# Mixing stage of a spectral layer: the filters of ScalarE and GpSimd are worked on one row ahead

## The chip, the cores and the metric

The kernel runs on one core of a Trainium2 chip. The metric is the device time of one execution in microseconds; the time of a kernel is the median over its runs. Engines are called TensorE (PE in the profile; PEld is its weight load), VectorE (DVE), ScalarE (ACT), GpSimd (POOL) and SyncE (SP), which here issues all DMAs.

## The reference

Two layers on x of shape (4, 128, 128, 128), float32: a state-space layer on windows of 8 x 8, and a spectral layer. The change touches a part of the second only. Cut to it:

```python
z = (x - mu) / sqrt(var + 1e-5) * ln_gamma + ln_beta
Xf = rfft2(z)                                  # b, d, 128, 65
Uf = Xf[:, :, None] * conj(Phi)                # 16 filters l, complex
U = irfft2(Uf)
S = einsum('bdlxy,lhd->bhxy', U, Theta)        # Theta: 16 matrices 128 x 128
H = gelu(einsum('bdxy,hd->bhxy', S, W1) + b1)
return x + einsum('bhxy,dh->bdxy', H, W2) + b2
```

The inverse transform is linear, so the kernel multiplies by Theta and sums over the 16 filters while the data are still spectra, and transforms back only the sum: for each frequency, S = sum over l of conj(Phi_l) * (Theta_l X), a complex product of a real matrix's result with a complex factor.

## The kernel before

The kernel has four stages, one after the other: `mamba_layer` (to about 7016 us of the span), `spectra` (forward transforms, to 7624), `mix` (to 9638) and `images_and_mlp` (inverse transforms and the two small matrices, to the end). Only `mix` changes.

`mix` goes over the 65 frequencies y of the halved axis, called rows here (KY is 65). A row's spectra, `xk`, are one tile of 128 channels by 4 images, 2 parts (real, imaginary) and 128 frequencies of the other axis. `load(y)` fetches it with two DMAs of 256 KB; the pool holds three such tiles, and the load of row y + 2 stands at the head of row y.

Within a row the loop runs over the 16 filters k (NL is 16). For each, TensorE makes two PSUM tiles v0 and v1 (line 578): Theta_k times the real and the imaginary part, each four matmuls of 128 x 128 x 128 in float32, one for each image. A tile fills one PSUM bank, and each of the two kinds has four buffers, so all eight banks are used. Then come four products with the factors Phi (`phi`, a column of 128 factors for every filter and row), each on 128 x 512 elements: real part from v0 and v1, imaginary part from v1 and v0.

Who works on the products depends on k:

- Ten filters are VectorE's. Line 593 makes the first two products of a row without an addition, line 595 multiplies a PSUM tile by its factor and adds the accumulator `acc`, all in one instruction.
- Six filters, APART = (1, 4, 6, 9, 12, 14), are ScalarE's and GpSimd's. ScalarE multiplies (line 589) from PSUM into a tile `part` in SBUF (eight buffers), and GpSimd adds it onto a second accumulator, `apart` in the code (line 591; the profile calls both accumulators acc). The first two products of a row are written straight into it, so a row has 24 products of ScalarE and 22 additions of GpSimd.

`finish(y)` (lines 557 to 564) adds the two accumulators of a row on VectorE (line 560, 128 x 1024) and stores the sum with eight DMAs of 64 KB. It stands behind filter 5 of the next row.

The stage has a manual schedule: every engine works through its instructions in the order in which the code writes them, and the semaphore waits between engines follow from the tiles. Which buffer of a tag a new tile gets is settled when the program is built; the pool does not simply take them in turn. A TensorE instruction that is to overwrite a bank waits for the engine that read the bank last.

Of the kernel before, what the change touches and what calls it, by code (L numbers as in the profile page):

```python
# [13 lines left out]
F32 = mybir.dt.float32  # L14
BF16 = mybir.dt.bfloat16
AF = mybir.ActivationFunctionType
ALU = mybir.AluOpType
PSUM = bass.MemoryType.PSUM

P = 128  # L20
# [6 lines left out]
W = 128  # L27
HB = 512
NL = 16
KY = W // 2 + 1  # L30
# [3 lines left out]
def mamba_layer(tc, d, x, x1, zb, deltas, dus):  # L34
# [14 lines left out]

    APART = {4: 0, 6: 2, 8: 5, 20: 12, 24: 15, 28: 18, 30: 26}  # L50
    rows_all = [(b, slice(i * WS, (i + 1) * WS)) for b in range(B) for i in range(NH)]
    R = len(rows_all)
    with ExitStack() as ctx:
# [79 lines left out]
        def take(slot, f):  # L133
            takes.setdefault(slot, []).append(f)
# [199 lines left out]
        def fetch(s):  # L334

            if 0 <= s < U * R:
                r, k = divmod(s, U)
                u = SimpleNamespace(o=rs[r], r=r, h=k // 16, ch=k // 8 % 2, i=k // 2 % 4, jp=k % 2, apart=k in APART)
                units[s] = u
# [18 lines left out]
        for r in range(R):  # L358
            for k, at in APART.items():
                take(U * r + at - 3, partial(fetch_du, U * r + k))  # L360
# [169 lines left out]
def mix(tc, d, xf, sf):  # L530

    nc = tc.nc
    B = len(sf)
    APART = (1, 4, 6, 9, 12, 14)
    with ExitStack() as ctx:
        ctx.enter_context(tc.manual_schedule())
        cp = ctx.enter_context(tc.tile_pool(name="m_const", bufs=1))
        sb = ctx.enter_context(tc.tile_pool(name="m_sb", bufs=3))  # L540
        ps = ctx.enter_context(tc.tile_pool(name="m_ps", bufs=4, space=PSUM))
        theta = cp.tile([P, NL, P], F32, tag="theta", name="theta")
        nc.sync.dma_start(theta, d["Theta"])
        phi = cp.tile([P, 3, NL, KY], F32, tag="phi", name="phi")
        nc.sync.dma_start(phi[:, 0], d["Phi_r"])
        nc.sync.dma_start(phi[:, 1], d["Phi_i"])
        nc.vector.tensor_scalar(phi[:, 2], phi[:, 1], -1.0, None, ALU.mult)
        rows = {}

        def load(y):  # L550
            if y < KY:
                rows[y] = o = SimpleNamespace()
                o.xk = sb.tile([P, B, 2, 2, W // 2], F32, tag="xk", name="xk")
                for q in range(2):
                    nc.sync.dma_start(o.xk[:, :, :, q], xf[y, :, :, q])

        def finish(y):
            if y >= 0:
                o = rows.pop(y)
                nc.vector.tensor_tensor(o.acc, o.acc, o.apart, ALU.add)  # L560
                at = y - 1 if 0 < y < KY - 1 else KY - 2 + y // (KY - 1)
                for b in range(B):
                    for q in range(2):
                        nc.sync.dma_start(sf[b][:, q, at], o.acc[:, b, :, q * (P // 2) : (q + 1) * (P // 2)])

        load(0)
        load(1)
        for y in range(KY):
            o = rows[y]
            load(y + 2)  # L570
            o.acc = sb.tile([P, B, 2, P], F32, tag="acc", name="acc")
            o.apart = sb.tile([P, B, 2, P], F32, tag="acc2", name="acc2")
            for k in range(NL):
                v = []
                for r in range(2):
                    t = ps.tile([P, B, P], F32, tag=f"v{r}", name=f"p_v{r}")
                    for b in range(B):
                        nc.tensor.matmul(t[:, b], o.xk[:, b, r], theta[:, k], start=True, stop=True)  # L578
                    v.append(t)
                for first in range(2):  # L580

                    for r, of, by in ((0, first, first), (1, 1 - first, 2 * first)):
                        factor = phi[:, by, k, y : y + 1]
                        mine, apart = o.acc[:, :, r], o.apart[:, :, r]
                        if k in APART:
                            part = apart
                            if k != APART[0] or first:
                                part = sb.tile([P, B, P], F32, tag="part", name="part", bufs=8)
                            nc.scalar.activation(part, v[of], AF.Copy, scale=factor)  # L589
                            if part is not apart:  # L590
                                nc.gpsimd.tensor_tensor(apart, apart, part, ALU.add)  # L591
                        elif k + first == 0:
                            nc.vector.tensor_scalar(mine, v[of], factor, None, ALU.mult)
                        else:
                            nc.vector.scalar_tensor_tensor(mine, v[of], factor, mine, ALU.mult, ALU.add)  # L595

                if k == 5:
                    finish(y - 1)
        finish(KY - 1)


# [108 lines left out]
@with_exitstack  # L710
def conv_kernel(ctx: ExitStack, tc: tile.TileContext, d, out):
    x = d["x"]
    B = x.shape[0]

    def images(name):
        return [tc.dram_tile([P, W, W], F32, name=f"{name}_{b}") for b in range(B)]

    x1, zb = images("x1"), images("z")
    xf = tc.dram_tile([KY, P, B, 2, 2, W // 2], F32, name="xf")
    sf = [tc.dram_tile([W, 2, KY, 2, P // 2], F32, name=f"sf_{b}") for b in range(B)]  # L720
    deltas, dus = (
        [[tc.dram_tile([P, WS * W], F32, name=f"{name}_{i}_{ch}") for ch in range(2)] for i in range(2)]
        for name in ("delta", "du")
    )
    mamba_layer(tc, d, x, x1, zb, deltas, dus)
    spectra(tc, d, zb, xf)
    mix(tc, d, xf, sf)
    images_and_mlp(tc, d, sf, x1, out)
# [70 lines left out]
```

## Time and profile before

| what | us |
|---|---|
| median of three runs | 10449.41 |
| lowest and highest run | 10445.54, 10451.61 |
| the profiled execution's own time | 10450.79 |
| its span, from the first to the last instruction | 10448.8 |
| stage `mix` within the span | 7624 to 9638 |

| busy time in the window 7624 to 9638 (2014 us) | us | instructions |
|---|---|---|
| TensorE, matmuls | 1941.4 | 16640 |
| TensorE, weight loads | 1883.2 | 16640 |
| VectorE | 1888.3 | 2665 |
| ScalarE | 987.6 | 1560 |
| GpSimd | 1829.3 | 1430 |

The granted TensorE clock in this window is 1.00 of full speed, and the DMA engines are busy 15% of it.

How to read it: a matmul of float32 leaves two records in the trace, so that one filter of one row has 16 (2 tiles x 4 images x 2) and a row has 256. A busy time is the union of an engine's instructions. A line of the timeline gives the start, the length, the engine, the line of the code, the operation, the tiles (written, then read) and the count of merged instructions; in brackets stands the idle time before it and what ended it. A line of the waits gives who waited for whom, the total in us, how many times, and the longest. In the windows each engine has its busy time and, in brackets, how many instructions began there.

### The profile page before, as it was taken

What the parts mean: (1) busy time and instruction counts of PE and PEld (TensorE: products, weight loads), DVE (VectorE), ACT (ScalarE), POOL (GpSimd) and SP (SyncE); (2) the same over time, 40 slices, a digit from 0 to 9 for tenths busy, and PEclk for the clock granted to TensorE, in tenths of its full rate; (3) what the DMA queues carried; (4) which work ended last, traced back from release to release, by engine and by line L of the source; (5) the groups of instructions that cost most, each with busy time, mean ns of one, the idle gap of its engine ahead of it and who ended that gap; (6) DMA issues with size and microseconds to landing.
All of it is one profiled execution on the core that took longest, in us unless ns stands there. A gap on an engine that the chain in (4) does not pass through costs nothing.

```text
span 10448.8 us, 143616 instructions
## 1 busy us (share of the span) xinstructions
PE 9293.9 (89%) x48900; PEld 5027.3 (48%) x48900; DVE 8980.1 (86%) x7234; ACT 6524.3 (62%) x12463; POOL 8231.4 (79%) x4188
## 2 busy tenths in 40 slices
PE   6888888888888888888888888887889999998999
PEld 2333333333333333333333333335889999998766
DVE  5999999999999999999999999995389999998433
ACT  5776777777777777777777677773344444444433
POOL 5899998998998998989989899893079999997000
PEclk8999989989999999999999999997999999999999
DMA  4777677777776776777767767775521111112332
GB/s 150 213 229 220 213 223 218 217 219 219 225 221 213 226 222 214 223 217 225 221 210 228 218 215 223 219 221 160 148 68 34 35 35 36 36 36 62 136 128 93
DMA packets 1168110, 1794.06 MB, mean 172 GB/s; under 512 B 368641, under 2 KB 436497, under 8 KB 1166225
## 3 DMA queue, kind: packets, MB, share of 16 engines
q1 hardware_dynamic: 1167376, 1784.88, 56.6%
q8 instruction: 387, 6.34, 0.3%
q14 instruction: 347, 2.83, 0.1%
HBM read 1481.44 MB, written 303.04 MB: 171 GB/s over the span
## 4 chain that ended last, share of the span: by engine, by line
PE 58%; ACT 20%; DVE 9%; DMA 7%; issue 4%; POOL 1%; SPq 1%; DVEq 0%; ACTq 0%; POOLq 0%
PE p_v L578 13%; DVE hs L410 6%; PE p_du L376 6%; PE p_conv L202 5%; DMA dr<-delta 5%; ACT part L589 5%; PE p_bc L217 5%; PE p_dt L227 4%; PE p_y L428 4%; DVE p_du L408 3%; PE p_out L274 2%; ACT dA L391 2%; PE ln_cen L150 2%; ACT p_du L391 2%; PE p_h L672 2%
## 5 line engine op out<-in xcount | busy, mean ns | idle before, releaser
L418 POOL TENSOR_TENSOR hs<-hs,bc 128x1024 f32<-128x1024 f32 x2048 | 4806.3, 2372 | 408.9 <-DVE hs L410 357.3
L410 DVE TENSOR_TENSOR_SCAN hs<-dA,p_du 128x1024 f32<-128x1024 f32 x1600 | 3659.0, 2287 | 208.2 <-DVE p_du L408 4.9
L591 POOL TENSOR_TENSOR acc<-acc,part 128x512 f32<-128x512 f32 x1430 | 1829.3, 1319 | 640.6 <-ACT part L589 640.6
L408 DVE TENSOR_TENSOR p_du<-p_du,bc 128x1024 f32<-128x1024 f32 x1600 | 1935.8, 1210 | 219.6 <-PE p_du L376 215.0
L391 ACT ACTIVATE dA<-dr,A 128x504 f32<-128x504 f32 x3200 | 2072.0, 704 | 33.1 <-DVE hs L410 23.7
L578 PE MATMUL p_v<-theta,xk 128*128 128x128 f32 x16640 | 1941.4, 277 | 87.9 <-ACT part L589 51.9
L578 PEld LDWEIGHTS p_v<-theta,xk 128*128 128x128 f32 x16640 | 1883.1, 192 | 146.2 <-ACT part L589 118.9
L595 DVE SCALAR_TENSOR_TENSOR acc<-p_v,phi,acc 128x512 f32<-128x512 f32 x2470 | 1672.4, 740 | 114.2 <-PE p_v L578 87.5
L376 PE MATMUL p_du<-du,c_rsel 32*128 32x512 f32 x6400 | 1364.3, 678 | 370.2 <-DVE hs L410 370.2
L589 ACT ACTIVATE part<-p_v,phi 128x512 f32<-128x512 f32 x1430 | 904.8, 686 | 803.9 <-PE p_v L578 800.3
L428 PE MATMUL p_y<-hs,c_ssel 128*32 128x512 f32 x8192 | 1225.7, 634 | 134.2 <-DVE yz L263 82.9
L410 DVE TENSOR_TENSOR_SCAN hs<-p_du,ur 128x1024 f32<-128x1024 f32 x448 | 1019.0, 2275 | 86.8 <-ACT p_du L391 60.5
L356 POOL TENSOR_TENSOR ur<-ur,bc 128x1024 f32<-128x1024 f32 x448 | 1063.1, 2373 | 10.7 <-DMA ur<-du 10.7
L202 PE MATMUL p_conv<-tn,W_conv 128*128 128x512 f32 x2048 | 1007.3, 616 | 3.2 <-ACT xc L207 1.6
L376 PEld LDWEIGHTS p_du<-du,c_rsel 32*128 32x128 f32 x6400 | 370.4, 192 | 1081.1 <-issue 780.6
L227 PE MATMUL p_dt<-xc,W_dt 128*128 128x512 f32 x1024 | 619.8, 736 | 48.0 <-ACT dl L238 42.3
L391 ACT ACTIVATE p_du<-dr,A 128x504 f32<-128x504 f32 x896 | 613.9, 685 | 29.1
L428 PEld LDWEIGHTS p_y<-hs,c_ssel 128*32 128x32 f32 x8192 | 184.3, 111 | 887.5 <-issue 571.2
L207 ACT ACTIVATE xc<-p_conv,b_conv 128x512 f32<-128x512 f32 x256 | 176.2, 688 | 639.3 <-PE p_conv L202 639.3
L245 POOL TENSOR_TENSOR dl<-dl,ab 128x1024 f32<-128x1024 f32 x128 | 302.6, 2364 | 338.5 <-ACT ab L242 338.5
L202 PEld LDWEIGHTS p_conv<-tn,W_conv 128*128 128x128 f32 x2048 | 346.8, 189 | 455.2 <-issue 247.9
L168 PE MATMUL ln_back<-ident,cs 128*128 128x128 f32 x2048 | 339.5, 316 | 222.3 <-ACT cs L162 216.6
(100 smaller groups left out, 10341.0 us busy)
## 6 DMA issues: line engine op xcount, KB each, us to landing
dr<-delta SPq DMA_DIRECT2D x4096, 256.0 KB, 5.2
ur<-du SPq DMA_DIRECT2D x896, 256.0 KB, 6.4
delta<-dl SPq DMA_DIRECT2D x128, 512.0 KB, 2.9
du<-du SPq DMA_DIRECT2D x128, 512.0 KB, 5.4
xf<-x SPq DMA_DIRECT2D x8, 4160.0 KB, 16.4
xk<-xf SPq DMA_DIRECT2D x130, 256.0 KB, 3.8
sf<-acc SPq DMA_DIRECT2D x520, 64.0 KB, 1.7
s<-sf SPq DMA_DIRECT2D x8, 4160.0 KB, 13.4
```

What stands on the lines that cost most here:

```text
L202: nc.tensor.matmul(windows(o.pc), W_conv[:, ch, k], moved, start=(k == 0), stop=(k == K - 1))
L356: nc.gpsimd.tensor_tensor(fetched[s], fetched[s], both(o.bc[0], h), ALU.mult)
L376: nc.tensor.matmul(u.bank[:, j % 2], c["rsel"][p, u.i], half(u.o.du[p, u.ch], u.h), start=True, stop=True)
L391: nc.scalar.activation(u.dA[:, q, :, 1:], u.delta[:, q].rearrange("p (w t) -> p w t", t=L)[:, :, 1:], AF.Exp, scale=A[:, g : g + 1],)
L408: nc.vector.tensor_tensor(u.bu, u.bu, both(u.o.bc[0], u.h), ALU.mult)
L410: nc.vector.tensor_tensor_scan(u.hs.rearrange("p q t -> p (q t)"), u.dA.rearrange("p q w t -> p (q w t)"), u.bu.rearrange("p q t -> p (q t)"),
L418: nc.gpsimd.tensor_tensor(u.hs, u.hs, both(u.o.bc[1], u.h), ALU.mult)
L428: nc.tensor.matmul(o.py[h, ch][32 * j : 32 * j + 32], c["ssel"][:, u.i], units[s + j // 2].hs[:, j % 2], start=(u.i == 0), stop=False, ski ...
L578: nc.tensor.matmul(t[:, b], o.xk[:, b, r], theta[:, k], start=True, stop=True)
L589: nc.scalar.activation(part, v[of], AF.Copy, scale=factor)
L591: nc.gpsimd.tensor_tensor(apart, apart, part, ALU.add)
L595: nc.vector.scalar_tensor_tensor(mine, v[of], factor, mine, ALU.mult, ALU.add)
```

## The change

The filters of ScalarE and GpSimd are now (0, 2, 5, 7, 10, 12), and in the loop over row y they are those of row y + 1: `ahead(y + 1, k)`. Their sum is made in the only accumulator that a row still has. VectorE's ten filters of row y, `mine(y, k)`, add onto it, the first product of the row included. In row 0 there is nothing made ahead, so VectorE works on all 16 filters of that row, beside the six of row 1; in the last row nothing is made ahead any more. The sum of the two accumulators in `finish` is gone. `xk` has four buffers, three rows are loaded at the start, and the load of row y + 3 stands behind `finish(y - 1)`, which itself stands behind filter 3 instead of filter 5.

```diff
--- before.py
+++ after.py
@@ -531,9 +531,11 @@
 
 
 
+
+
     nc = tc.nc
     B = len(sf)
-    APART = (1, 4, 6, 9, 12, 14)
+    APART = (0, 2, 5, 7, 10, 12)
     with ExitStack() as ctx:
         ctx.enter_context(tc.manual_schedule())
         cp = ctx.enter_context(tc.tile_pool(name="m_const", bufs=1))
@@ -550,52 +552,64 @@
         def load(y):
             if y < KY:
                 rows[y] = o = SimpleNamespace()
-                o.xk = sb.tile([P, B, 2, 2, W // 2], F32, tag="xk", name="xk")
+                o.xk = sb.tile([P, B, 2, 2, W // 2], F32, tag="xk", name="xk", bufs=4)
                 for q in range(2):
                     nc.sync.dma_start(o.xk[:, :, :, q], xf[y, :, :, q])
+
+        def products(o, k):
+            v = []
+            for r in range(2):
+                t = ps.tile([P, B, P], F32, tag=f"v{r}", name=f"p_v{r}")
+                for b in range(B):
+                    nc.tensor.matmul(t[:, b], o.xk[:, b, r], theta[:, k], start=True, stop=True)
+                v.append(t)
+
+            return [(v[of], r, by) for first in range(2) for r, of, by in ((0, first, first), (1, 1 - first, 2 * first))]
+
+        def ahead(y, k):
+            if y == KY:
+                return
+            o = rows[y]
+            if k == APART[0]:
+                o.acc = sb.tile([P, B, 2, P], F32, tag="acc", name="acc")
+            for i, (v, r, by) in enumerate(products(o, k)):
+                into = part = o.acc[:, :, r]
+                if k != APART[0] or i >= 2:
+                    part = sb.tile([P, B, P], F32, tag="part", name="part", bufs=8)
+                nc.scalar.activation(part, v, AF.Copy, scale=phi[:, by, k, y : y + 1])
+                if part is not into:
+                    nc.gpsimd.tensor_tensor(into, into, part, ALU.add)
+
+        def mine(y, k):
+            o = rows[y]
+            if y + k == 0:
+                o.acc = sb.tile([P, B, 2, P], F32, tag="acc", name="acc")
+            for i, (v, r, by) in enumerate(products(o, k)):
+                into, factor = o.acc[:, :, r], phi[:, by, k, y : y + 1]
+                if y + k == 0 and i < 2:
+                    nc.vector.tensor_scalar(into, v, factor, None, ALU.mult)
+                else:
+                    nc.vector.scalar_tensor_tensor(into, v, factor, into, ALU.mult, ALU.add)
 
         def finish(y):
             if y >= 0:
                 o = rows.pop(y)
-                nc.vector.tensor_tensor(o.acc, o.acc, o.apart, ALU.add)
                 at = y - 1 if 0 < y < KY - 1 else KY - 2 + y // (KY - 1)
                 for b in range(B):
                     for q in range(2):
                         nc.sync.dma_start(sf[b][:, q, at], o.acc[:, b, :, q * (P // 2) : (q + 1) * (P // 2)])
 
-        load(0)
-        load(1)
+        for y in range(3):
+            load(y)
         for y in range(KY):
-            o = rows[y]
-            load(y + 2)
-            o.acc = sb.tile([P, B, 2, P], F32, tag="acc", name="acc")
-            o.apart = sb.tile([P, B, 2, P], F32, tag="acc2", name="acc2")
             for k in range(NL):
-                v = []
-                for r in range(2):
-                    t = ps.tile([P, B, P], F32, tag=f"v{r}", name=f"p_v{r}")
-                    for b in range(B):
-                        nc.tensor.matmul(t[:, b], o.xk[:, b, r], theta[:, k], start=True, stop=True)
-                    v.append(t)
-                for first in range(2):
-
-                    for r, of, by in ((0, first, first), (1, 1 - first, 2 * first)):
-                        factor = phi[:, by, k, y : y + 1]
-                        mine, apart = o.acc[:, :, r], o.apart[:, :, r]
-                        if k in APART:
-                            part = apart
-                            if k != APART[0] or first:
-                                part = sb.tile([P, B, P], F32, tag="part", name="part", bufs=8)
-                            nc.scalar.activation(part, v[of], AF.Copy, scale=factor)
-                            if part is not apart:
-                                nc.gpsimd.tensor_tensor(apart, apart, part, ALU.add)
-                        elif k + first == 0:
-                            nc.vector.tensor_scalar(mine, v[of], factor, None, ALU.mult)
-                        else:
-                            nc.vector.scalar_tensor_tensor(mine, v[of], factor, mine, ALU.mult, ALU.add)
-
-                if k == 5:
+                if k not in APART or y == 0:
+                    mine(y, k)
+                if k in APART:
+                    ahead(y + 1, k)
+                if k == 3:
                     finish(y - 1)
+                    load(y + 3)
         finish(KY - 1)
```

## The prediction

> **What bounds the kernel now.** I read the page's slices first, then the windows, the waits and the timeline of the mixing stage alone, since the diff touches nothing else. The stage runs from 7624.0 us (first matmul) to 9632.1 us (end of the last sum of a row), 2008 us for 65 rows, 30.9 us a row. The windows show one steady row (the second line) beside three early ones (the first).
>
> ```profile
> core 0: us, PE busy (x) PEld busy (x) DVE busy (x) ACT busy (x) POOL busy (x), PEclk, DMA share, GB/s
> 7640.00:7732.00 92.00, 91.92 (x824) 91.72 (x822) 91.10 (x131) 48.97 (x78) 89.66 (x71) 1.00 0.15 34
> 8525.07:8555.96 30.89, 29.91 (x257) 28.96 (x257) 29.08 (x42) 15.20 (x24) 28.16 (x23) 1.00 0.16 35
> ```
>
> To be seen: in the steady row four engines are at 91 to 97%, none at 100. In the early rows TensorE has no gap at all and its granted clock is still 1.00. The waits of the stage name one repeated gap:
>
> ```profile
> PEld p_v L578 <- ACT part L589: 118.9, 305, 0.7
> ```
>
> That is 305 times, 0.39 us each. TensorE's timeline shows their shape; the first line is the start of the stage, the next five are the steady row and the restart after it.
>
> ```profile
> 7624.04 107.87 PE L578 MATMUL p_v<-theta,xk 128*128 128x128 f32 x944 [27.15 <-DMA xk<-xf]
> ...
> 8525.07 9.20 PE L578 MATMUL p_v<-theta,xk 128*128 128x128 f32 x80 [0.21 <-ACT part L589]
> 8534.47 5.62 PE L578 MATMUL p_v<-theta,xk 128*128 128x128 f32 x48 [0.21 <-ACT part L589]
> 8540.31 3.84 PE L578 MATMUL p_v<-theta,xk 128*128 128x128 f32 x32 [0.21 <-ACT part L589]
> 8544.35 11.40 PE L578 MATMUL p_v<-theta,xk 128*128 128x128 f32 x96 [0.21 <-ACT part L589]
> 8555.96 9.20 PE L578 MATMUL p_v<-theta,xk 128*128 128x128 f32 x80 [0.21 <-ACT part L589]
> ```
>
> A filter k of a row (I say a pair: tiles v0 and v1) is 16 matmul records, a row 256. Pipelined records come every (9.20 - 3.84) / (80 - 32) = 0.1117 us, so a pair takes 1.787 us (call it a slot) and a row 28.6. The row takes 30.89, so 2.29 us go in five restarts of 0.458 each (0.21 of gap, 0.26 of filling again; the fifth lies inside the x96). Check on the stage: 1040 pairs x 1.787 + 305 x 0.458 + 2.1 for the slow first pairs (944 records took 107.87, 2.1 more than 944 x 0.1117 and one fill) = 2000.3; measured 2002 to the last matmul. So TensorE's rate and 305 restarts make the stage.
>
> Why it restarts is in the built program, which fixes the PSUM bank of every tile: 305 of the 1040 pairs are put into the bank pair that ScalarE emptied of the pair two before, exactly the count of the waits; others come back after three (ScalarE) or four to six (VectorE). ScalarE's last eviction of the pair that began at 8525.07 ends at 8527.22 + 1.84 = 8529.06, 3.99 us after it, in this line:
>
> ```profile
> 8527.22 1.84 ACT L589 ACTIVATE part<-p_v,phi 128x512 f32<-128x512 f32 x3 [0.21 <-PE p_v L578]
> ```
>
> Two slots are 3.57 us: too short by 0.4. Three are 5.36: 1.4 to spare. In rows 0 to 2 no pair has a distance of two, and these rows show the price without restarts; VectorE's sums of rows start 28.59 and 28.58 us apart there:
>
> ```profile
> 7667.83 2.29 DVE L560 TENSOR_TENSOR acc<-acc,acc 128x1024 f32<-128x1024 f32 x1
> ...
> 7696.42 2.28 DVE L560 TENSOR_TENSOR acc<-acc,acc 128x1024 f32<-128x1024 f32 x1
> ...
> 7725.00 2.28 DVE L560 TENSOR_TENSOR acc<-acc,acc 128x1024 f32<-128x1024 f32 x1
> ```
>
> The other prices, from VectorE's and GpSimd's timelines (20 products; 22 additions of rows 0 and 1, beside which no sum of a row runs) and from the tile view of acc (min/median/max ns):
>
> ```profile
> 8529.07 13.25 DVE L595 SCALAR_TENSOR_TENSOR acc<-p_v,phi,acc 128x512 f32<-128x512 f32 x20
> ```
>
> ```profile
> 7635.41 27.15 POOL L591 TENSOR_TENSOR acc<-acc,part 128x512 f32<-128x512 f32 x22 [1.44 <-ACT part L589]
> ```
>
> ```profile
> L591 POOL TENSOR_TENSOR acc<-acc,part x1430: 1253/1274/2287, 7631.5 to 9629.5; 128x512 f32<-128x512 f32 x179
> L560 DVE TENSOR_TENSOR acc<-acc,acc x65: 1225/2273/2295, 7667.8 to 9630.8; 128x1024 f32<-128x1024 f32 x65
> ```
>
> A product is 0.66 us in a row of them (2.64 a pair, 1.48 slots), an addition of GpSimd 1.234, the sum of a row 2.27.
>
> **What the Trainium skill says.** "Perfetto Trace Analysis", section Optimization Strategy: the same gap repeating on the engine that should be saturated can mean too little PSUM for the next tile; its section Matmuls wants independent groups to rotate through banks so that the eviction of one overlaps the next. The trace agrees (305 gaps of 0.39 us), with the refinement that it is the order of rotation that falls short: with the same eight banks rows 0 to 2 have no gap. "SBUF — State Buffer", section Who interferes with whom: a VectorE instruction with two SBUF inputs and a GpSimd instruction that reads SBUF block each other; with at most one SBUF input VectorE doesn't. The trace agrees: the sum of a row takes 1225 ns when GpSimd is done and 2273 beside it, one addition per row stretches to 2287, while a product, which has one input in PSUM, keeps to 733 to 754 ns all along.
>
> **The change part by part.**
> 1. The sum of a row (65 x 2.27 = 148 us of VectorE) goes. In steady rows VectorE idles 1.8 us (30.89 - 29.08), so alone this gains nothing; but at 28.6 a row VectorE would have no slack (40 x 0.66 + 2.27 = 28.7). Without it: 26.4. GpSimd loses the stretched addition, 1.0 us a row: 22 x 1.234 = 27.1. ScalarE stays near 15.2.
> 2. The bank plan changes with the order. In the changed program 10 pairs have a ScalarE distance of two, all in rows up to 5; the rest wait on ScalarE at three or four, on VectorE at four to six. So 295 restarts go: 295 x 0.458 = 135 us. What is late next, in slots from the row's start, with VectorE's pairs in slots 1, 3, 4, 6, 8, 9, 11, 13, 14, 15: walking them at 1.48 slots each, a pair is done at most 3.3 after its start (slot 15, at 18.3); its banks are wanted at 4 or 5. Margin 0.7 slot, 1.3 us. I cost it at nothing; if it's wrong, each restart left per row costs 64 x 0.458 = 29 us.
> 3. VectorE's first product of a row gains a wait on GpSimd; queued behind it are that row's other 39, and TensorE through the banks. ScalarE's pairs are in slots 0, 2, 5, 7, 10, 12; walking the additions (0.69 slot each, first part 2 slots after a pair starts), those of slot 12 run from 14.35 to 17.1. VectorE reaches the product at 18.3. Margin 2 us: nothing, as long as an addition stays near 1.234.
> 4. Loads of xk go three rows ahead instead of two, on SP now behind the eight stores of the finished row (their issue takes 4 us). A load lands in 3.8 us and is first read over one row later, 28 us: nothing. Without that cover a row would wait for it, as the first does.
> 5. Row 0 holds 22 pairs, 16 of them VectorE's: 39.3 us of TensorE, 42.2 of VectorE. VectorE ends up to 4 slots behind, at distances of 5 and 6 there: I take nothing, at most 3 us. It makes up 2.2 us a row afterwards.
> 6. The last row has ten pairs, all VectorE's: 40 x 0.66 = 26.4 us sets the end, not the 17.9 of TensorE.
> 7. At the end three loads of constants, issued before the last stores until now, stand behind them: 3 x 0.43 us on SP, and their bytes ahead of the next stage's first load. I take +1.5, between 0 and 3.
>
> Sum: the last row's first pair starts after 22 + 63 x 16 = 1030 pairs: 1030 x 1.787 + 10 x 0.458 + 2.1 = 1847.3; VectorE starts it 2.3 us later and needs 26.5: 7624.0 + 1876.1 = 9500.1 against 9632.1, -132.0. The same arithmetic came out 1.7 short of the stage before: +1.7. Tail +1.5. In all -128.8. The profiled execution took 10450.79 us (span 10448.8 and 2.0 around it): 10322.0. The median of the runs is 1.4 below that execution: 10320.6, say 10320.
>
> **Rivals.**
> - Restarts remain (2 above): ScalarE held up by its eight part buffers, or VectorE's margin of 1.3 us used up. For: the three pairs 13 to 15 in a row; GpSimd at 95% of 28.6. Against: part buffers of eight additions before are free by the walk above over a slot ahead. Two a row left: 10380.
> - TensorE's granted clock gives way when it never pauses. For: 0.93 over the first 7016 us. Against: 1.00 in 7640 to 7732 at 91.92 us busy of 92. At 0.927, where the gain of rows 1 to 63 is gone, row 0 and the last row remain: 10460, the same within 0.2%. The change not having its effect on restarts at all gives about this, too.
> - Slower: GpSimd sets the row. Every product of a row now waits for its 22 additions to be done a row earlier, which until now only the sum of a row needed, six slots into the next row. It decides when an addition, stretched by a neighbour, exceeds (30.89 - 1.5 of idle before the first part) / 22 = 1.335 us. At 1.40 a row takes 32.3: 63 x 1.4 and some 10 for the first and last rows, 10550. Against: 1.234 beside products in rows 0 and 1.
>
> **How the numbers follow.** Forecast 0.83, at 10308 to 10350 (a measurement can tell about 0.2%, 21 us, from no change). Restarts left 0.09 (10380), clock or no effect 0.04 (10460), GpSimd 0.04 (10550). The range 10308 to 10350 leaves 0.17 to these; its lower end is a tail of 0 and a lead of VectorE smaller than 2.3 with no restart, its upper end row 0 at 3, the tail at 3, and nearly one restart a row. Faster by over 0.2%: 0.92; within: 0.04; slower: 0.04.
>
> **What would show it.** Right: steady rows of 28.6 us with TensorE busy throughout at clock 1.00; waits of weight loads on ScalarE near 10; L591's maximum below 1.4 us; VectorE idle about 2 us a row behind TensorE. Wrong: VectorE waiting on GpSimd before a row's first product, TensorE waiting on VectorE, a clock under 0.98, or a row of 22 additions over 28.6.

## The result, and the profile after

| | before | changed |
|---|---|---|
| median of four runs, us | 10447.69 | 10320.54 |
| lowest and highest run | 10445.54, 10451.61 | 10315.76, 10328.00 |
| profiled execution, its span | 10450.79, 10448.8 | 10328.00, 10326.2 |

The ratio is 0.9881, with a 95% interval of 0.9865 to 0.9896: 127 us less, 10320.54 against 10320 predicted. That the two agree to within 1 us is luck: the four runs of the changed kernel lie 12 us apart.

The windows of the changed kernel, for one steady row (columns as in the windows of before):

```profile
8500.00:8528.60 28.60, 28.60 (x259) 28.60 (x258) 27.00 (x41) 15.21 (x26) 27.22 (x23) 1.00 0.17 38
```

TensorE and its weight loads are now busy for the whole row, at a granted clock of 1.00, and the row takes 28.6 us instead of 30.89. VectorE has 1.6 us to spare, GpSimd 1.4. The waits of the stage (who waited for whom, us, times, longest):

```profile
POOL acc L581 <- ACT part L579: 565.9, 102, 470.1
...
DVE acc L592 <- PE p_v L564: 80.9, 132, 1.5
...
PEld p_v L564 <- ACT part L579: 3.7, 10, 0.4
...
PE p_v L564 <- DVE acc L592: 2.7, 5, 0.6
```

Call it a return after two when a pair is given the banks that the pair two before it held. The built program before has 305 such returns behind ScalarE, the changed one 10, and the wait of the weight loads for ScalarE came 305 times before and 10 times now. VectorE never waits for GpSimd; it waits for TensorE. TensorE's timeline shows where the rest of the waits lie:

```profile
7628.41 33.23 PE L564 MATMUL p_v<-theta,xk 128*128 128x128 f32 x272 [27.01 <-DMA xk<-xf]
7661.85 5.62 PE L564 MATMUL p_v<-theta,xk 128*128 128x128 f32 x48 [0.21 <-ACT part L579]
...
7714.60 1770.30 PE L564 MATMUL p_v<-theta,xk 128*128 128x128 f32 x15840 [0.21 <-ACT part L579]
9485.18 2.02 PE L564 MATMUL p_v<-theta,xk 128*128 128x128 f32 x16 [0.28 <-DVE acc L592]
...
9495.72 2.02 PE L564 MATMUL p_v<-theta,xk 128*128 128x128 f32 x16 [0.61 <-DVE acc L592]
```

One stretch of 15840 of the 16640 records takes 1770.3 us: 0.1118 us a record, the rate that the rows of before gave between two restarts. The last lines are the last row, in which VectorE works alone and TensorE waits for it. The tile view of acc (min/median/max ns) shows what became of the stretched additions:

```profile
L592 DVE SCALAR_TENSOR_TENSOR acc<-p_v,phi,acc x2622: 736/743/753, 7632.9 to 9505.4; 128x512 f32<-128x512 f32 x188
L581 POOL TENSOR_TENSOR acc<-acc,part x1408: 1257/1278/1330, 7636.2 to 9476.6; 128x512 f32<-128x512 f32 x176
```

No addition of GpSimd exceeds 1330 ns any more; one in every row had come near 2287.

Where the time went, between the two profiled executions: the stage, from its first matmul to VectorE's last instruction, went from 2008.0 us to 9505.4 + 0.74 - 7628.41 = 1877.7, so 130.3 less. From there to the first matmul of the next stage it took 2.0 us more (22.8 against 20.8), the last stage 1.3 more, and the two stages ahead 4.4 more, although nothing in them changed: in the profiles of this study the first matmul of `mix` lay anywhere from 7618.4 to 7632.3. Together -122.6, the difference of the spans; the medians say -127.

### The profile page after: what moved, and what is told of

The parts are those of the page before. It is cut to its first block, busy times and chain, and to the rows that moved or that the text cites. A ratio compares the mean times of both kernels' runs of the same rounds, so it can differ in the third digit from the quotient of the medians.

```text
span 10326.2 us, 144410 instructions
## 1 busy us (share of the span) xinstructions
PE 9221.1 (89%) x48900; PEld 5007.4 (48%) x48900; DVE 8861.2 (86%) x7193; ACT 6509.4 (63%) x12439; POOL 8141.9 (79%) x4166
## 4 chain that ended last, share of the span: by engine, by line
PE 65%; ACT 15%; DVE 8%; DMA 7%; issue 3%; SPq 1%; POOL 1%; DVEq 0%; ACTq 0%; POOLq 0%
PE p_v L564 18%; PE p_conv L202 6%; PE p_du L376 6%; DVE hs L410 5%; DMA dr<-delta 5%; PE p_dt L227 5%; PE p_bc L217 5%; PE p_y L428 5%; PE p_out L274 2%; DVE p_du L408 2%; ACT dA L391 2%; PE ln_cen L150 2%; ACT p_du L391 2%; PE p_h L686 2%; PE p_o L695 2%
## 5 line engine op out<-in xcount | busy, mean ns | idle before, releaser
L410 DVE TENSOR_TENSOR_SCAN hs<-dA,p_du 128x1024 f32<-128x1024 f32 x1600 | 3659.0, 2287 | 208.6 <-DVE p_du L408 4.9
L581 POOL TENSOR_TENSOR acc<-acc,part 128x512 f32<-128x512 f32 x1408 | 1740.9, 1280 | 570.9 <-ACT part L579 565.9
L564 PE MATMUL p_v<-theta,xk 128*128 128x128 f32 x16640 | 1864.8, 275 | 31.5 <-DMA xk<-xf 27.0
L564 PEld LDWEIGHTS p_v<-theta,xk 128*128 128x128 f32 x16640 | 1861.9, 192 | 34.4 <-issue 27.2
L592 DVE SCALAR_TENSOR_TENSOR acc<-p_v,phi,acc 128x512 f32<-128x512 f32 x2622 | 1767.8, 743 | 105.4 <-PE p_v L564 80.9
```

The costliest lines, as they stand in the source:

```text
L410: nc.vector.tensor_tensor_scan(u.hs.rearrange("p q t -> p (q t)"), u.dA.rearrange("p q w t -> p (q w t)"), u.bu.rearrange("p q t -> p (q t)"),
L581: nc.gpsimd.tensor_tensor(into, into, part, ALU.add)
L592: nc.vector.scalar_tensor_tensor(into, v, factor, into, ALU.mult, ALU.add)
```

## Experiments

The theory: a row of this stage is TensorE's 28.6 us plus 0.46 for each return after two, and nothing else of the change counts for more than a few us. Rival A: the relief of VectorE and GpSimd from the sum of a row is the gain. Rival C: the gain needs the six filters made a row ahead. The change does all three at once, the order of the banks, the sum and the filters ahead, so each was done by itself.

**e1_before_round: only the order of the banks, on the kernel before.**

```diff
+        made = []
+
+        def banks(apart):
+            made.append(len(made) % 4)
+            return made[-1]
...
+                s = banks(k in APART)
                 for r in range(2):
-                    t = ps.tile([P, B, P], F32, tag=f"v{r}", name=f"p_v{r}")
+                    t = ps.tile([P, B, P], F32, tag=f"v{r}{s}", name=f"p_v{r}", bufs=1)
```

> The kernel before, all its work kept, the sum of a row too; only the PSUM banks are given out in strict turn (every pair comes back after four). Theory (the gain is the restarts, and the order of banks alone makes them): weight loads no longer wait for ScalarE 305 times, a row goes from 30.9 to 28.6 or 28.7 us (VectorE: 40 x 0.66 + 2.27 = 28.7), so 10448 - 139 = about 10309. Rival A (the gain is VectorE's and GpSimd's relief from the sum of a row): nothing changes, 10448. Rival B (with the sum kept, VectorE falls more than four pairs behind and TensorE waits for it instead): a row of 29 to 29.5 us, 10335 to 10365.

Measured: 10309.75 us, ratio 0.9865 (0.9848 to 0.9881). TensorE's timeline of this run, and then its windows:

```profile
7632.34 1860.79 PE L585 MATMUL p_v<-theta,xk 128*128 128x128 f32 x16640 [27.17 <-DMA xk<-xf]
```

```profile
8500.00:8600.00 100.00, 100.00 (x898) 100.00 (x897) 100.00 (x144) 53.18 (x84) 98.30 (x77) 1.00 0.17 38
```

All 1040 pairs in one stretch, without a gap. VectorE, which still makes the sum of every row, is busy 100 of 100 us beside TensorE, and it is just enough. So the whole gain is to be had from the banks alone, with the sum kept and no filter made ahead. Rival A falls, and so does rival B of the expectation.

**e3_before_nosum: only the sum away, the banks as they were.** The output lacks the share of six filters.

```diff
-                nc.vector.tensor_tensor(o.acc, o.acc, o.apart, ALU.add)
...
+        back = (2, 6, 5, 2, 5, 5, 2, 5, 5, 3, 5, 2, 5, 5, 2, 5)
...
+            n = len(made)
+            made.append((2, 3, 1, 3, 0, 2, 0, 1, 3, 0, 2, 0, 1, 3, 1, 2)[n] if n < 16 else made[n - back[n % 16]])
```

> The kernel before without the sum of a row on VectorE, with the order of its banks kept as it was in its steady rows (324 returns after two pairs, 305 before). The output lacks the share of ScalarE's and GpSimd's six filters. Theory: VectorE just idles 2.3 us more in a row; with 19 more restarts of 0.458 us the time is 10448 + 9 = about 10457. Rival A (VectorE's and GpSimd's relief is the gain): 64 x 2.27 = 145 us less, 10303.

Measured: 10453.25 us, ratio 1.0006 (0.9997 to 1.0014). The waits of its weight loads:

```profile
PEld p_v L586 <- ACT part L597: 126.4, 324, 0.7
```

148 us of VectorE's work are gone and the time is the same: work of an engine that was waiting for TensorE anyway. Its windows say so, too; VectorE is busy 88% of the time (94% in the steady row of before, 29.08 of 30.89 us), TensorE 97% as before:

```profile
8500.00:8600.00 100.00, 96.85 (x832) 93.80 (x831) 88.25 (x130) 49.35 (x78) 87.06 (x71) 1.00 0.15 33
```

**e8_before_nosum_free: the sum away, the banks left to the pool.** The same edit without the table, so that the output lacks the same share.

```diff
-                nc.vector.tensor_tensor(o.acc, o.acc, o.apart, ALU.add)
```

> The kernel before without the sum of a row on VectorE, and the order of banks left to the pool, which then has no return after two pairs at all. The output lacks the share of ScalarE's and GpSimd's six filters. Theory: no restarts, rows of 28.6 us, 10448 - 140 = about 10308, that is at least the changed kernel's time without any filter made ahead. Rival C (making them a row ahead is what frees TensorE): 10448.

Measured: 10304.98 us, ratio 0.9863 (0.9849 to 0.9878). TensorE's timeline has no gap in the stage:

```profile
7628.01 1860.76 PE L577 MATMUL p_v<-theta,xk 128*128 128x128 f32 x16640 [27.27 <-DMA xk<-xf]
```

From e3 it differs in the order of the banks alone, and by 148 us. Rival C falls: no filter was made ahead. And it shows by what the change reached the banks: with the sum gone from the program the pool by itself gives no bank back after two pairs.

**e2_after_two: the changed kernel with the banks given back after two pairs.**

```diff
+        def banks(apart):
+            if len(made) >= 4:
+                oldest = min(range(4), key=lambda s: max(i for i, (t, _) in enumerate(made) if t == s))
+                s = made[-2][0] if made[-2][1] and made[-1][0] != made[-2][0] else oldest
+            else:
+                s = len(made)
+            made.append((s, apart))
+            return s
...
```

> The changed kernel, all its work kept, with banks given out so that a pair takes those of the pair two before whenever ScalarE had it (383 times, 10 in the changed kernel). Theory: six restarts in a row, a row of 28.6 + 6 x 0.458 = 31.35 us, in all 373 x 0.458 = 171 us more than 10320: about 10491, slower than the kernel before. Rival A (the relief of VectorE and GpSimd is the gain): about 10320.

Measured: 10488.42 us, ratio to the kernel before 1.0041 (1.0026 to 1.0056). The waits of its weight loads:

```profile
PEld p_v L576 <- ACT part L591: 149.9, 383, 0.7
```

Everything else that the change does is in this kernel, and it is slower than before. 168 us over the changed kernel for 373 more returns: 0.45 us each, as priced.

**e4_after_sum and e4r_after_sum_round: the sum put back into the changed kernel, with the pool's banks and in strict turn.** The sum is of the old size but on spare tiles, on which nothing waits. The second kernel has the edit of e1 besides.

```diff
+        spare = [cp.tile([P, B, 2, P], F32, tag=f"spare{i}", name="spare") for i in range(2)]
...
                 o = rows.pop(y)
+                nc.vector.tensor_tensor(spare[1], spare[0], spare[1], ALU.add)
```

> The changed kernel with a sum of the same size as before (128 x 1024, two SBUF inputs) put back on VectorE once a row, on spare tiles; the order of banks is left to the pool, which then gives 380 returns after two pairs instead of 10. Theory (the sum matters only because the pool, with it in the program, hands ScalarE's banks out again at once): 370 x 0.458 = 169 us more than 10320, about 10490. Rival A (the sum costs its own time): 65 x 2.27 = 148 us at most on VectorE, of which 2 a row are idle in the changed kernel: 10325 to 10340.

> The same as e4_after_sum, with the banks given out in strict turn. Theory: no restarts; the sum's own time is left. VectorE has 656 pairs x 2.64 + 65 x 2.27 = 1879 us, 19 more than TensorE's 1860, so it sets the stage: some 4 to 8 us more than the changed kernel's stage, about 10327. If the sum as such undid the gain: over 10440.

Measured: 10496.12 us (1.0044, 1.0027 to 1.0061) and 10321.15 us (0.9878, 0.9863 to 0.9892). The waits of the first:

```profile
PEld p_v L567 <- ACT part L582: 148.9, 380, 0.7
```

One instruction of 2.3 us a row costs 176 us in all if the pool orders the banks, and next to nothing if they go in turn: from the first matmul of the stage to the first of the next it is 1896.9 us with the sum and 1895.3 without (e5 below). It isn't its time: in the changed kernel, too, it is what the presence of this instruction does to the pool's order. For the second kernel I had expected VectorE to set the stage, at 6 us more; it did not, since a sum took 1.29 us there and not 2.27 (see the last section), and VectorE still had time to wait for TensorE in nearly every row (63 waits, 33.6 us). Why the pool hands ScalarE's banks out again at once when the sum is in the program stays open: what is shown is the order in the built programs, not the reason.

**e6_after_oldk: a row ahead, but at the old filters.** A test of the wait that the change adds.

```diff
-    APART = (0, 2, 5, 7, 10, 12)
+    APART = (1, 4, 6, 9, 12, 14)
```

> The changed kernel with the filters of ScalarE and GpSimd where they were (1, 4, 6, 9, 12, 14), still a row ahead, so that GpSimd's last addition of a row (slot 18.5) comes after the slot of VectorE's first product (16.6), which has to wait for it. Theory: VectorE waits 1.9 slots, 3.4 us a row, but its pairs then end at most 4.0 slots after they began, just within the distance of the banks; TensorE hardly notices: 10320 to 10350. Rival D (the wait for GpSimd goes straight into the row, so that the choice of filters 0, 2, 5, 7, 10, 12 is what the gain hangs on): 64 x 3.4 = 218 us more, 10540.

Measured: 10325.92 us, ratio 0.9882 (0.9867 to 0.9896). VectorE's waits, and the windows:

```profile
DVE acc L592 <- POOL acc L581: 128.5, 126, 1.8
```

```profile
8500.00:8600.00 100.00, 100.00 (x898) 100.00 (x898) 91.74 (x139) 53.12 (x85) 94.42 (x77) 1.00 0.18 41
```

Now VectorE does wait for GpSimd, 2.0 us a row, and TensorE still has no gap in the steady rows: the wait is paid out of VectorE's own slack. Rival D falls; the new places of the filters keep a wait away that wouldn't have been felt.

**e7_pool2: two more additions a row on GpSimd.**

```diff
+        spare = [cp.tile([P, B, P], F32, tag=f"spare{i}", name="spare") for i in range(2)]
...
+            if k in APART[-2:]:
+                nc.gpsimd.tensor_tensor(spare[1], spare[0], spare[1], ALU.add)
```

> The changed kernel with two more additions of 128 x 512 a row on GpSimd, on spare tiles: 24 of 1.242 us. This tests from where on GpSimd sets the row. The prediction's formula, 22 x d + 1.5 us of idle before a row's first part: 24 x 1.242 + 1.5 = 31.3 us a row, 63 x 2.7 = 170 us more: 10490. If the idle time vanishes once GpSimd is behind: 29.8 us, 63 x 1.2 = 76 us more: 10396. If GpSimd isn't near the path: 10320.

Measured: 10377.64 us, ratio 0.9934 (0.9919 to 0.9949). A row of it in the windows:

```profile
8519.44:8549.02 29.58, 28.94 (x258) 28.74 (x257) 26.53 (x41) 15.61 (x24) 29.58 (x25) 1.00 0.16 37
```

GpSimd is busy without a pause and sets the row: 29.58 / 24 = 1.233 us an addition. The first form of the expectation, with 1.5 us of idle in each row, is wrong: once GpSimd is behind, it doesn't wait for a row's first part. The second form had 76 us more than the changed kernel; 57 were measured. The weight loads of this kernel wait for ScalarE 10 times, as in the changed kernel, so spare tiles and more additions on GpSimd do not by themselves move the banks as the sum on VectorE does.

**e5_after_round, e9_round_again, e10_after_again: the ranking, on one chip.** e5 is the changed kernel with banks in strict turn (its edit is that of e1), e9 is e1 again, e10 the changed kernel as it is.

> The changed kernel with the banks given out in strict turn: its last 10 returns after two pairs go (4.6 us). 10320 - 5 = about 10315; if VectorE's pairs of row 0 (up to 4 slots late) then meet a bank after four, that is given back: 10320.

> e1_before_round once more, beside the changed kernel on one chip, to rank the two: by its trace its stage is 11.6 us shorter than the changed kernel's (no row of 22 pairs at the start, no row at the end in which VectorE works alone): about 10309.

> The changed kernel as it is, beside the two others on one chip: about 10320.

Measured: 10314.16 us (10311.26 to 10317.25), 10308.17 (10304.80 to 10315.58) and 10320.65 (10318.94 to 10324.50); the ratios to the kernel before are 0.9868, 0.9863 and 0.9874, each with an interval of about 0.0015 on either side. The runs of e9 and e10 don't overlap: the old kernel with its banks in turn beats the changed one by 12 us. From the first matmul of the stage to the first of the next, e9 needs 1888.2 us, e5 1895.3, e10 1898.8, the kernel before 2028.8. What separates e5 from e9 is the price of working ahead: of the 7.1 us some 5 lie before VectorE's last instruction of the stage, since TensorE waits for it in the last row, which VectorE has to itself, and 2 behind it, as in part 7 of the prediction.

## Why the prediction was right, step by step

- **The bound.** 0.1117 us a record, 0.458 a restart, 305 of them: e1 (1860.8 us for the 1040 pairs without a restart, against 1040 x 1.787 + 2.1 = 1860.6) and e2 (0.45 for each restart put in) measured both terms alone.
- **The sum of a row, part 1.** "Alone this gains nothing" holds for its time (e3: 1.0006). As an edit it is wrong: alone it gives everything (e8), through the pool. I had compared the banks of the two programs only, and not asked which edit moved them.
- **The bank plan, part 2.** The count (10) and the price were right. The sentence that the plan "changes with the order" is the step that failed: with the sum in the program the old order has 305 returns and the new one 380 (e4), without it the old order has none (e8) and the new one 10. The sum's presence decides, so the number came out right from a count made on the built program, with the wrong edit named as its cause. That nothing else comes late next held: in rows 1 to 63 TensorE does not wait for VectorE at all.
- **The new wait, part 3.** There is no wait of VectorE for GpSimd in the changed kernel. e6 shows that the margin of 2 us wasn't even needed. There I expected 3.4 us of wait a row and it was 2.0.
- **The loads, part 4.** TensorE waits for xk once, at the start of the stage, 27.0 us, as before.
- **The first and the last row, parts 5 and 6.** Row 0 is the first 352 records, that is the stretches of 272 and 48 and part of the next; the gaps between them are waits for ScalarE, none for VectorE. The last row ends with VectorE; the stage took 1877.7 us, the sum said 1876.1.
- **The tail, part 7.** +1.5 was +2.0.
- **The rivals.** The clock stayed at 1.00 with TensorE busy throughout. The price of GpSimd's rival was wrong: e7 shows a row of 24 x 1.233 without idle. By an estimate from that, GpSimd takes TensorE's place from 28.6 / 22 = 1.30 us an addition, and only at 30.89 / 22 = 1.40 would the gain of the steady rows be gone; I had put that point at 1.335, and 1.40 at 100 us slower than before.

## What to carry to other kernels

When an engine that should be saturated shows one short gap again and again, count the gaps and compare the count with the order in which the built program reuses its buffers, before any work is moved off other engines: here an equal count (305) named the cause, and one tag for each bank was worth as much as a rewrite. Where a pool chooses buffers, an edit can act through that choice alone; fix the order by hand and repeat the edit, to learn what the edit itself is worth. And a wait added to an engine with slack in every row can cost nothing (e6), while work beyond the slack sets the row (e7).

## What the runs showed of the hardware

Who is held up when a sum of VectorE with both inputs in SBUF meets an addition of GpSimd differs from kernel to kernel. The tile views of e4 and then e4r (min/median/max ns), the same instruction at the same place in the code:

```profile
L600 DVE TENSOR_TENSOR spare<-spare x65: 1211/2268/2282, 7676.5 to 9674.9; 128x1024 f32<-128x1024 f32 x65
...
L584 POOL TENSOR_TENSOR acc<-acc,part x1408: 1257/1278/1356, 7631.7 to 9643.0; 128x512 f32<-128x512 f32 x176
```

```profile
L607 DVE TENSOR_TENSOR spare<-spare x65: 1211/1287/1385, 7674.7 to 9496.9; 128x1024 f32<-128x1024 f32 x65
```

```profile
L591 POOL TENSOR_TENSOR acc<-acc,part x1408: 1257/1279/2274, 7630.0 to 9467.2; 128x512 f32<-128x512 f32 x176
```

In e4 VectorE loses 1 us a row and GpSimd none, in e4r it is the other way round, and in the kernel before both were stretched (2273 and 2287 ns in the prediction's tile view). It fits what the Trainium skill says ("SBUF — State Buffer", section Who interferes with whom: the two engines share a pair of ports as an exclusive lock, and the order in which they issue decides who is blocked). So the price of such a sum can't be carried from one kernel to the next. That the order of issue is what differs between these kernels is argued, not shown.
